# A graph-network layer on one core: norms begun later behind their load, stores issued by ScalarE, four first inputs loaded together, a second lane half a batch behind

## The chip, the cores and the metric

The kernel runs on one core of a Trainium2 chip. The metric is device time in microseconds, median of several runs. The core has a TensorE (matmuls and transposes; PE in the profile, with PEld for its weight loads), a VectorE (DVE), a ScalarE (ACT), a GpSimd (POOL) and a sync engine (SP) that here does nothing but issue transfers. Each engine has its own instruction stream and takes it in order; semaphores make one wait for another.

## The reference

Input x has 32 batches of 512 nodes with 256 channels; adj holds a 512 x 512 mask for each batch. Everything is float32.

```python
h = maximum(layernorm(x), 0)                       # over the channels
out = x + layer(h, adj)

def layer(x, mask):                                # x is h here
    xc = transpose(x, (0, 2, 1))
    c = relu(bn1(conv1d(xc, conv1_w, 0)))          # 1 tap
    c = bn2(conv1d(c, conv2_w, 8))                 # 17 taps
    x_conv = transpose(relu(c + xc), (0, 2, 1))
    s = x @ w_se.T + b_se                          # 3 numbers per node
    dist = |s_n|^2 + |s_m|^2 - 2 s_n.s_m
    A = exp(-dist) * mask
    msg = relu(x @ w_msg.T + b_msg)
    x_nmp = A @ msg
    gi = concat(x_conv, x_nmp) @ w_ih.T + b_ih     # 3 x 256 outputs
    gh = x @ w_hh.T + b_hh
    r, z = sigmoid(gi_r + gh_r), sigmoid(gi_z + gh_z)
    n = tanh(gi_n + r * gh_n)
    return (1 - z) * n + z * x
```

## The kernel before

All the work of a batch lies on 128 partitions; a 512 x 256 array is four chunks of 128 nodes (NT = 4), or, transposed, two halves of 128 channels (ND = 2). A batch passes through these stages, each a Python generator that emits instructions and yields the time it plans for them on TensorE:

- `begin(b)`: `norm_t` transposes the normalized input on TensorE, half by half, into PSUM (`ps_tr`, two buffers), and ScalarE writes it with a ReLU to `hT` (line 241, two buffers). After the second half `hT` is stored to DRAM (`hd`, line 244), for later stages that read it again, and the input of batch b + 2 is loaded into one of two `x_sb` buffers (line 100). Its norm is put on a list at once (line 617).
- `norm(b)`: VectorE takes statistics of the four chunks (lines 213 and 214), GpSimd raises variance + eps to the power -0.5 (line 147, result `rstd`), VectorE subtracts and scales in place (line 221). It is a generator of five pieces, which are taken one at a time between other work.
- `rows(b)`: the 1-tap convolution (`conv1`) into `h1`, for groups of G = 4 batches.
- `graph(lane, b)`: `messages` (four pairs of matmuls, line 519, recorded at line 93; VectorE takes the result out of PSUM at lines 520 and 521), `factors` and `factors_t`, `kernel_exp` (four small matmuls and four exponentials on ScalarE into `at`), `masked` (the mask tile is transposed on TensorE and multiplied in by VectorE, line 570), and `gather` (eight matmuls, result copied by ScalarE to `xnmp`, line 582, and stored to DRAM as `nd`, line 583).
- `convolution`: the 17-tap convolution as 25 matrix products (`ps_c`) for each group of four batches, by an algorithm with fewer multiplications. Its operands come from sums on VectorE (lines 261 and 264), its 25 weight tiles are computed once in the front (`weights_first`, stored to DRAM as `wd`, line 359) and loaded again for each group (line 365). It starts when all 25 are made and the second lane has no batches left.
- `gates(b)`: 48 matmuls with the two gate weights `whh` and `wih` (line 670), with sigmoids and tanh on ScalarE and a mix on GpSimd, then `finish` (transposes back, residual, store).

There are two lanes for graphs. Lane 0 has buffers for the whole run and takes batches 0, 2, 4 and all from 6; lane 1 has batches 1, 3 and 5 and lives in a pool `prep`, which is closed when the convolution starts, so that the `late` pool (gate weights and buffers) can take its space (`late_pools`).

The order of instructions on every engine is written out by a small planner at the end: each stage is a stream with a rate and a starting clock, and the stream with the lowest clock that is ready goes next. After each step `pace` hands VectorE and ScalarE pieces of side work, as far as a credit allows: sums, operands, norms, weight preparation, evacuations. A piece of a norm is taken as soon as the norm is on the list; nothing asks whether its input has landed. All transfers, loads and stores, are issued by the sync engine in program order.

Of the kernel before, what the change touches and what calls it, by code (L numbers as in the profile page):

```python
# [8 lines left out]
F32 = mybir.dt.float32  # L9
# [4 lines left out]
P = 128  # L14
# [17 lines left out]
G = 4  # L32
# [10 lines left out]
def kernel(  # L43
# [27 lines left out]
    nc = tc.nc  # L71
    B, N, D = x.shape
    NT = N // P
# [7 lines left out]
    front = ctx.enter_context(tc.tile_pool(name="front", bufs=2))  # L81
# [13 lines left out]

    XS, HB, HR, XN, XR = {}, {}, {}, {}, {}

    def load(b):
        XS[b] = front.tile([P, NT, D], F32, name="x_sb", bufs=2)
        nc.sync.dma_start(XS[b], x[b].rearrange("(c p) d -> p c d", p=P))  # L100

    def load_row(b):
# [98 lines left out]
    HT = {}  # L201
    HD = {b: dram.tile([P, ND, N], F32, name=f"hd{b}") for b in range(B)}
    ND_ = {(b, d): dram.tile([P, N], F32, name=f"nd{b}_{d}") for b in range(B) for d in range(ND)}

    NORMS = {}

    def norm(b):

        xs = XS[b]
        st = front.tile([P, NT, 6], F32, name="st")  # L210
        mv = front.tile([P, NT, 2], F32, name="mv")
        for c in range(NT):
            nc.vector.bn_stats(st[:, c, :], xs[:, c, :])  # L213
            nc.vector.bn_aggr(mv[:, c, :], st[:, c, :])  # L214
            if c % 2:
                yield
        rstd = front.tile([P, NT], F32, name="rstd")
        rsqrt(rstd, mv[:, :, 1])
        yield
        for c in range(NT):  # L220
            nc.vector.tensor_scalar(
                xs[:, c, :], xs[:, c, :], mv[:, c, 0:1], rstd[:, c : c + 1],
                op0=ALU.subtract, op1=ALU.mult,
            )
            if c % 2:
                yield

    def norm_all(b):
        if b in NORMS:
            for _ in NORMS.pop(b):  # L230
                pass

    def norm_t(b, d):
        xn = XS[b]
        if d == 0:
            norm_all(b)
            HT[b] = front.tile([P, ND, N], F32, name="hT", bufs=2)
        ps = tr.tile([P, N], F32, name="ps_tr")
        for c in range(NT):
            nc.tensor.transpose(ps[:, c * P : (c + 1) * P], xn[:, c, d * P : (d + 1) * P], ident)  # L240
        nc.scalar.activation(HT[b][:, d, :], ps, AF.Relu)  # L241
        if d == ND - 1:
            XS.pop(b)
            nc.sync.dma_start(HD[b], HT[b])

    def conv1(b, o):
        hT = HT[b] if b < G else HR[b]
# [80 lines left out]
    def weights_first():  # L328

        nonlocal made_w  # L330
        outer = [
            taps_of(
                lambda k, i=i: wraw[:, i, :, :, k, :],
                lambda i=i: prep.tile([P, 2, 3, D], F32, name=f"g{i}", bufs=1),
                True,
            )
            for i in range(ND)
        ]
        for j1 in ORDER:
            g = []  # L340
            for o in outer:
                g.append(next(o))
                yield
            inner = [
                taps_of(
                    lambda k, i=i: g[i][:, :, k, :],
                    lambda i=i: prep.tile([P, 2, D], F32, name=f"gg{i}", bufs=2),
                    False,
                )
                for i in range(ND)  # L350
            ]
            for j2 in ORDER:
                w = cv.tile([P, 2, ND, D], F32, name="w", bufs=3)
                for i in range(ND):
                    nc.scalar.activation(
                        w[:, :, i, :], next(inner[i]), AF.Copy, scale=GSCALE[j1] * GSCALE[j2]
                    )
                    yield
                nc.sync.dma_start(WD[made_w], w)
                made_w += 1  # L360

    def weights_again():
# [107 lines left out]
    def convolution():  # L470

        nonlocal at_product
        wg = (w for _ in range(NG) for w in weights_again())
        yield lambda: made_w == 25 and not lanes[1].batches
        late_pools()
        for g in range(NG):
            sums = summed(g)
            next(sums)
            done = None
            for n in range(25):  # L480
                at_product = m = 25 * g + n
                while len(WS) < min(m + 1 + AHEAD_W, 25 * NG):
                    WS.append(next(wg))
                while len(X2) < m + 1:
                    while operand_some() is None:
                        yield lambda: made > g
                w, x2 = WS[m], X2[m].rearrange("p (r v) -> p r v", v=V)
                ps = cps.tile([P, N], F32, name="ps_c")[:, :NZ]
                for o in range(ND):
                    matmul_sum(  # L490
                        ps[:, o * NU : (o + 1) * NU].rearrange("p (b u) -> p b u", u=U),
                        [
                            (w[:, k, i, o * P : (o + 1) * P], x2[:, i * G : (i + 1) * G, k : k + U])
                            for k in range(2)
                            for i in range(ND)
                        ],
                    )
                    if o == 0 and done is not None:
                        sums.send(done)
                    yield 1.71  # L500
                WS[m] = X2[m] = None
                done = ps
            sums.send(done)


    def late_pools():
        nonlocal late, wih, whh
        prep_ctx.close()
        late = ctx.enter_context(tc.tile_pool(name="late", bufs=1))
        whh = late.tile([P, ND, 3 * D], F32, name="whh")  # L510
        wih = late.tile([P, 2 * ND, 3 * D], F32, name="wih")
        nc.sync.dma_start(whh, w_hh)
        nc.sync.dma_start(wih, w_ih)

    wih = whh = None

# [32 lines left out]
    def kernel_exp(lane, at):  # L549

        pss = []
        for c in range(NT // 2):
            pss += [lane.ps(), tr.tile([P, N], F32, name="ps_tr")]
        for c in range(NT):
            k = slice(32 * c, 32 * c + 5)
            nc.tensor.matmul(  # L556
                pss[c], lane.left[k, :], lane.right[k, :], start=True, stop=True,
                tile_position=(32 * c, 0),
            )
        for c in range(NT):  # L560
            nc.scalar.activation(at[:, c, :], pss[c], AF.Exp)
# [11 lines left out]
    def gather(lane, b, msg, at, d):  # L573
        ps = lane.ps()
        for c in range(NT):
            nc.tensor.matmul(  # L576
                ps, msg[:, c, d * P : (d + 1) * P], at[:, c, :], start=(c == 0), stop=(c == NT - 1)
            )
            if c == 1:
                yield 1.73  # L580
        xnmp = front.tile([P, N], F32, name="xnmp", bufs=1)
        nc.scalar.activation(xnmp, ps, AF.Copy)
        nc.sync.dma_start(ND_[b, d], xnmp)
        yield 1.73

    def finish(b, o_sb, c):
# [20 lines left out]
    def begin(b):  # L607

        nonlocal begun
        yield lambda: begun == b and (b < 2 or b - 2 in messaged) and (b - 2 >= G or made_rows >= b - 1)  # L610
        for d in range(ND):
            norm_t(b, d)
            if d == ND - 1:
                begun = b + 1
                if b + 2 < B:
                    load(b + 2)
                    NORMS[b + 2] = norm(b + 2)
            yield 0.55, 2.0 * d

    made_rows = 0  # L620
# [10 lines left out]
    def graph(lane, b):  # L631

        msg = lane.pool.tile([P, NT, D], F32, name="msg", bufs=1)
        at = lane.pool.tile([P, NT, N], F32, name="at", bufs=1)
        for c in range(NT):
            messages(lane, b, msg, c)
            if c == NT - 1:
                factors(lane)
                messaged.add(b)
            yield 0.93, 0.0 if c < NT - 1 else 4.5  # L640
        factors_t(lane)
        yield 0.67, 3.0
        kernel_exp(lane, at)
        yield 1.2, 5.5
        for n in range(NT):
            masked(lane, b, at, n)
            yield 0.55, 1.0 if n < NT - 1 else 2.5
        for d in range(ND):
            yield from gather(lane, b, msg, at, d)
# [147 lines left out]
    def all_graphs(lane):  # L797
        for b in list(lane.batches):
            if b < G:
                yield lambda: begun > b  # L800
            else:
                yield from begin(b)
            yield from graph(lane, b)
        lane.batches = []
# [10 lines left out]
            yield from rows(b)  # L815

    def all_gates():
        yield lambda: late is not None
        for b in range(B):
            yield from gates(b)  # L820

    NORMS[0] = norm(0)
    load(1)
    NORMS[1] = norm(1)
    lanes[0].ask(3)
    lanes[1].ask(2)
    for k0, k1 in ((0, 9), (9, TAPS)):
# [7 lines left out]
        "finish": (all_finishes(), 1e9, -2.0),  # L835
        "rows": (all_rows(), 1e9, -2.0),
        "graphs": (all_graphs(lanes[0]), 63.0, -1.4),
        "other graphs": (all_graphs(lanes[1]), 63.0, -1.4),
        "conv": (convolution(), 85.5, 0.0),
        "gates": (all_gates(), 125.0, 1.1),  # L840
    }
# [77 lines left out]
```

## Time and profile before

| | |
|---|---|
| time, median of 3 | 2545.94 us (2544.59 to 2547.88) |
| span in the profile | 2541.5 us |
| mean granted TensorE clock | 0.952 of full speed |
| VectorE idle before line 213 for an x load | 274.2 us in 25 waits |
| x load, 512 KB | 4.9 us from issue to landing (median) |
| first matmul of the convolution | at 237.86 us |
| first gate matmul | at 446.41 us |
| bytes moved | 292.56 MB, 115 GB/s over the span |

A row of the profile names engine, source line, operation, output and inputs, the count, the busy time and the idle time of the engine just before, with what ended it (the releaser). "L93" is a helper that records every matmul of `matmul_sum`, so messages, 1-tap convolution and the 17-tap products all have it and are told apart by their tiles: `ps_g<-wmsg,hT` (or `ps_acc` in lane 1) are messages, `ps_c` are products. The clock of TensorE is given as a share of full speed for a stretch. The chain that ended last is followed back from the last instruction and says which work set the end.

The run has a front of some 238 us (six graphs, four rows, the weight preparation), a middle in which convolution, graphs and gates are interleaved, and an end from about 2390 us with gates alone.

### The profile page before, as it was taken

How to read it: one execution, taken by the hardware profiler on the slowest of the kernel's cores; microseconds unless marked ns; L12 is line 12 of the kernel's file. 1: busy time of each engine (PE TensorE's matmuls, PEld its weight loads, DVE VectorE, ACT ScalarE, POOL GpSimd, SP SyncE). 2: the span in 40 equal slices, each digit the busy share in tenths (PEclk: the TensorE clock that was granted, in tenths of full speed). 3: DMA queues.
4: the chain of work that ended last, by engine and by line, in shares of the span. 5: the costliest groups of instructions: out<-in, count | busy, mean ns of one | idle time of the engine just before them, and what ended most of it. 6: DMA issues, size and time to landing. Idle time of an engine off the chain costs nothing.

```text
span 2541.5 us, 21847 instructions
## 1 busy us (share of the span) xinstructions
PE 2316.6 (91%) x8224; PEld 1460.6 (57%) x8224; DVE 1181.6 (46%) x1989; ACT 648.3 (26%) x936; POOL 350.4 (14%) x242
## 2 busy tenths in 40 slices
PE   4667998988889998999999998999999999999998
PEld 2335766555556565666556655666666666666543
DVE  4753755444254443545436544445545554565211
ACT  1432223222222322232222411223221311311211
POOL 1000000110011111101102110111111221121222
PEclk8768999999989999999999999999999999999999
DMA  4543444233333333333323333332333332423221
GB/s 168 190 165 137 153 153 157 83 101 115 124 108 104 120 99 108 129 112 116 113 98 125 112 119 114 124 124 78 118 116 103 112 117 91 133 83 100 83 66 33
DMA packets 136312, 292.56 MB, mean 115 GB/s; under 512 B 12432, under 2 KB 61968, under 8 KB 135568
## 3 DMA queue, kind: packets, MB, share of 16 engines
q1 hardware_dynamic: 136208, 291.18, 34.1%
q8 instruction: 65, 1.06, 0.2%
q14 instruction: 39, 0.32, 0.0%
HBM read 227.69 MB, written 63.44 MB: 115 GB/s over the span
## 4 chain that ended last, share of the span: by engine, by line
PE 80%; DVE 7%; DMA 5%; issue 4%; ACT 2%; POOL 1%; SPq 0%; POOLq 0%; ACTq 0%; DVEq 0%
PE ps_acc L670 37%; PE ps_c L93 22%; PE ps_g L576 7%; PE ps_g L93 7%; DMA x_sb<-in_x_dram 5%; PE ps_tr L568 2%; DVE st L213 1%; PE ps_g L556 1%; PE ps_tr L590 1%; PE ps_acc L576 1%; ACT hT L241 1%; DVE mv L214 1%; PE ps_tr L544 1%; PE ps_tr L240 0%; DVE xconv L680 0%
## 5 line engine op out<-in xcount | busy, mean ns | idle before, releaser
L93 PE MATMUL ps_c<-x,w 128*128 128x228 f32 x3200 | 683.1, 361 | 16.4 <-DMA w<-wd 14.4
L93 PEld LDWEIGHTS ps_c<-x,w 128*128 128x128 f32 x3200 | 608.5, 193 | 135.4 <-issue 106.3
L670 PE MATMUL ps_acc<-xconv,wih 128*128 128x512 f32 x768 | 365.5, 599 | 10.5 <-ACT xconv L681 10.5
L670 PE MATMUL ps_acc<-xnb,wih 128*128 128x512 f32 x768 | 361.4, 593 | 0.0
L670 PE MATMUL ps_acc<-hTb,whh 128*128 128x512 f32 x768 | 358.9, 597 | 0.0
L707 POOL TENSOR_TENSOR o_sb<-hTb,r 128x512 f32<-128x512 f32 x64 | 103.6, 1619 | 1446.0 <-ACT r L702 1391.9
L701 DVE TENSOR_TENSOR r<-ps_acc,r 128x512 f32<-128x512 f32 x64 | 44.3, 691 | 474.1 <-PE ps_acc L670 474.1
L93 PE MATMUL ps_g<-wmsg,hT 128*128 128x259 f32 x464 | 143.2, 454 | 110.3 <-DVE aug L521 80.9
L670 PEld LDWEIGHTS ps_acc<-xconv,wih 128*128 128x128 f32 x768 | 143.8, 193 | 147.8 <-issue 132.7
L670 PEld LDWEIGHTS ps_acc<-hTb,whh 128*128 128x128 f32 x768 | 145.0, 192 | 142.1 <-issue 137.6
L670 PEld LDWEIGHTS ps_acc<-xnb,wih 128*128 128x128 f32 x768 | 142.6, 190 | 140.7 <-issue 140.2
L576 PE MATMUL ps_g<-at,msg 128*128 128x512 f32 x464 | 214.5, 601 | 0.6 <-DVE at L570 0.6
L93 PEld LDWEIGHTS ps_g<-wmsg,hT 128*128 128x128 f32 x464 | 101.6, 226 | 151.3 <-issue 136.0
L213 DVE BATCH_NORM_STATS2 st<-x_sb 128x6 f32<-128x256 f32 x128 | 51.6, 403 | 274.2 <-DMA x_sb<-in_x_dram 274.2
L264 DVE SCALAR_TENSOR_TENSOR x<-x,x 128x471 f32<-128x471 f32 (+1 forms) x184 | 168.9, 918 | 3.1
L261 DVE TENSOR_TENSOR x<-x 128x471 f32<-128x471 f32 x200 | 165.8, 846 | 0.1
L576 PEld LDWEIGHTS ps_g<-at,msg 128*128 128x128 f32 x464 | 89.0, 193 | 101.4 <-issue 99.3
L692 DVE SCALAR_TENSOR_TENSOR r<-ps_acc,vec,r 128x512 f32<-128x512 f32 x64 | 48.0, 750 | 211.9 <-PE ps_acc L670 209.5
L570 DVE TENSOR_TENSOR at<-ps_tr,at 128x512 f32<-128x512 f32 x128 | 87.7, 688 | 120.7 <-PE ps_tr L568 113.8
L147 POOL TENSOR_TENSOR rstd<-veps,mhalf 128x4 f32<-128x4 f32 x32 | 38.1, 1190 | 726.4 <-DVE veps L146 726.4
L698 ACT ACTIVATE z<-ps_acc,brz 128x512 f32<-128x512 f32 x64 | 44.0, 687 | 324.2 <-PE ps_acc L670 320.2
L524 ACT ACTIVATE msg<-msg 128x512 f32<-128x512 f32 x64 | 40.2, 628 | 290.6 <-DVE msg L520 290.6
(105 smaller groups left out, 2195.7 us busy)
## 6 DMA issues: line engine op xcount, KB each, us to landing
w<-wd SPq DMA_DIRECT2D x200, 512.0 KB, 3.7
m_sb<-in_adj_dram SPq DMA_DIRECT2D x128, 256.0 KB, 2.7
x_sb<-in_x_dram SPq DMA_DIRECT2D x32, 512.0 KB, 4.9
hd<-hT SPq DMA_DIRECT2D x32, 512.0 KB, 3.0
nd<-xnmp SPq DMA_DIRECT2D x64, 256.0 KB, 2.0
hTb<-hd SPq DMA_DIRECT2D x32, 512.0 KB, 4.5
xnb<-nd SPq DMA_DIRECT2D x64, 256.0 KB, 3.0
res<-in_x_dram SPq DMA_DIRECT2D x64, 256.0 KB, 3.9
```

Of the source, the lines that this page charges most:

```text
L93: nc.tensor.matmul(ps, lhsT, rhs, start=(i == 0), stop=(i == len(pairs) - 1))
L213: nc.vector.bn_stats(st[:, c, :], xs[:, c, :])
L261: nc.vector.tensor_tensor(dst, get(a), get(b), op=ALU.subtract)
L264: nc.vector.scalar_tensor_tensor(dst, a, -2.0, b, op0=ALU.mult, op1=ALU.add)
L568: nc.tensor.transpose(ps[:, c, :], m[:, c * P : (c + 1) * P], ident)
L570: nc.vector.tensor_tensor(part, ps, part, op=ALU.mult)
L576: nc.tensor.matmul(ps, msg[:, c, d * P : (d + 1) * P], at[:, c, :], start=(c == 0), stop=(c == NT - 1))
L670: nc.tensor.matmul(ps, w[:, at + i, cols(o, g)], hT[:, i, :] if k == 0 else x_in[2 * k - 2 + i], start=(k == of[0] and i == 0), stop=(k == ...
L692: nc.vector.scalar_tensor_tensor(r, ps_h, vec[:, _COL["b_hh"] + 2 * ND + o : _COL["b_hh"] + 2 * ND + o + 1], r, op0=ALU.add, op1=ALU.mult,)
L698: nc.scalar.activation(z, ps_z, AF.Sigmoid, bias=brz[:, ND + o : ND + o + 1])
L701: nc.vector.tensor_tensor(r, ps_n, r, op=ALU.add)
L707: nc.gpsimd.tensor_tensor(t, hT[:, o, :], r, op=ALU.subtract)
```

## The change

Four edits, and one number of the planner.

1. A norm is no longer put on the list when its load is issued. `norm_begin` is called after the exponentials of a graph, for the next two batches not yet begun, and by `norm_t` for a batch that nobody has begun. It is meant to let the load land before VectorE meets the norm.
2. The first four inputs are loaded at the start, two of them into the space of lane 1's `at` buffer; so `at` is taken later, and the graphs of batches 0 to 3 wait at that point until batch 3 has been transposed. Batches 4 and 5 are loaded after the transposes of 0 and 1.
3. The stores of `hT`, of `xnmp` and of the prepared weights are issued by ScalarE, which has just written the data, in place of the sync engine.
4. The gate weights are loaded when the convolution has come to product 3, and not ahead of its first weights; the gates stream waits for that.
5. The second lane's clock starts at -1.27 in place of -1.4, half a batch behind the first.

```diff
-    def load(b):
-        XS[b] = front.tile([P, NT, D], F32, name="x_sb", bufs=2)
+    def load(b, xs=None):
+        XS[b] = front.tile([P, NT, D], F32, name="x_sb", bufs=2) if xs is None else xs
...
+    def norm_begin(b):
+        if b < B and b not in normed:
+            normed.add(b)
+            NORMS[b] = norm(b)
...
         if d == 0:
+            if b not in normed:
+                norm_begin(b)
             norm_all(b)
...
-            nc.sync.dma_start(HD[b], HT[b])
+            nc.scalar.dma_start(HD[b], HT[b])
...
-                nc.sync.dma_start(WD[made_w], w)
+                nc.scalar.dma_start(WD[made_w], w)
...
+                if m == 3:
+                    nc.sync.dma_start(whh, w_hh)
+                    nc.sync.dma_start(wih, w_ih)
...
-        nc.sync.dma_start(whh, w_hh)
-        nc.sync.dma_start(wih, w_ih)
...
-        nc.sync.dma_start(ND_[b, d], xnmp)
+        nc.scalar.dma_start(ND_[b, d], xnmp)
...
-                if b + 2 < B:
-                    load(b + 2)
-                    NORMS[b + 2] = norm(b + 2)
+
+                later = b + 4 if b < 2 else b + 2 if b >= G else B
+                if later < B:
+                    load(later)
...
-        at = lane.pool.tile([P, NT, N], F32, name="at", bufs=1)
...
+        if b < G:
+            yield lambda: begun >= G
+        at = lane.pool.tile([P, NT, N], F32, name="at", bufs=1)
         kernel_exp(lane, at)
+        norm_begin(begun)
+        norm_begin(begun + 1)
...
-        yield lambda: late is not None
+        yield lambda: at_product > 3
...
-    NORMS[0] = norm(0)
     load(1)
-    NORMS[1] = norm(1)
+    spare = prep.tile([P, NT, N], F32, name="at", bufs=1).rearrange("p c (k d) -> p (c k) d", d=D)
+    for b in (2, 3):
+        load(b, spare[:, (b - 2) * NT : (b - 1) * NT, :])
+    for b in range(G):
+        norm_begin(b)
...
-        "other graphs": (all_graphs(lanes[1]), 63.0, -1.4),
+        "other graphs": (all_graphs(lanes[1]), 63.0, -1.27),
```

More of the change, by code (lines that the diff above doesn't have):

```diff
@@ L203 @@
     ND_ = {(b, d): dram.tile([P, N], F32, name=f"nd{b}_{d}") for b in range(B) for d in range(ND)}
-    NORMS = {}
+    NORMS, normed = {}, set()
+    def norm_begin(b):
+        if b < B and b not in normed:
+            normed.add(b)
+            NORMS[b] = norm(b)
     def norm(b):
```

## The prediction

> **What bounds the kernel now.** I read the shares of busy time first, then the table of stretches, the waits, the chain that ended last, and one stall in order of time.
>
> ```profile
> PE 2316.6 (91%) x8224; PEld 1460.6 (57%) x8224; DVE 1181.6 (46%) x1989; ACT 648.3 (26%) x936; POOL 350.4 (14%) x242
> PEclk8768999999989999999999999999999999999999
> ```
>
> TensorE is the bound, 91% busy; what can be won is its 225 us of idle time and the time it runs at a reduced clock. Both are early: the slices of the clock below 9 are the first four and one more. Two 40 us stretches of the middle, with a stall and without (columns: busy us and count of PE, PEld, DVE, ACT, POOL, then clock, DMA share, GB/s):
>
> ```profile
> 270.00:310.00 40.00, 34.06 (x148) 27.20 (x147) 24.89 (x48) 7.36 (x14) 1.32 (x1) 0.91 0.36 125
> 350.00:390.00 40.00, 40.00 (x172) 28.28 (x171) 15.64 (x18) 11.44 (x19) 0.00 (x0) 1.00 0.42 147
> ```
>
> Where there is no stall, PE has no idle time at all and the full clock. The waits, whole run (us in total, times, longest):
>
> ```profile
> DVE st L213 <- DMA x_sb<-in_x_dram: 274.2, 25, 22.2
> PE ps_g L93 <- DVE aug L521: 80.9, 17, 7.3
> PE ps_g L93 <- DVE veps L146: 29.4, 5, 6.8
> PE ps_tr L540 <- issue: 16.4, 1, 16.4
> PE ps_c L93 <- DMA w<-wd: 14.4, 1, 14.4
> PE ps_acc L93 <- DVE veps L146: 10.6, 1, 10.6
> PE ps_acc L670 <- ACT xconv L681: 10.5, 5, 4.7
> ```
>
> The message matmuls (line 93, called from line 519) wait 110 us in 22 pieces for VectorE to free their PSUM, and VectorE waited 25 times for an x load. The timeline shows that these are one thing (start us, length, engine, line, operation, then idle before it and its releaser):
>
> ```profile
> 280.02 0.32 SPq L244 DMA_DIRECT2D hd<-hT  x1
> 280.43 0.38 SPq L100 DMA_DIRECT2D x_sb<-in_x_dram  x1
> ...
> 282.12 1.92 PE L93 MATMUL ps_g<-wmsg,hT 128*128 128x259 f32 x8
> 285.32 0.43 DVE L213 BATCH_NORM_STATS2 st<-x_sb 128x6 f32<-128x256 f32 x1 [12.04 <-DMA x_sb<-in_x_dram]
> ...
> 289.35 0.42 DVE L520 TENSOR_TENSOR msg<-ps_g,bmsg 128x256 f32<-128x256 f32 x1
> ...
> 289.98 3.79 PE L93 MATMUL ps_g<-wmsg,hT 128*128 128x259 f32 x8 [5.94 <-DVE aug L521]
> ```
>
> The load is issued at 280.43. The norm's first instruction follows it in VectorE's program and blocks VectorE until 285.3; then come 2.1 us of statistics and some sums, and only at 289.35 does VectorE take the messages out of PSUM. PE stands 5.94 us, and then 8 matmuls take 3.79 us, where the 8 before the stall took 1.92. The chain that ended last counts the load itself as 5% of the span and lines 213 and 214 as 1% each.
>
> **What the Trainium skill says.** "TensorE: Matmul & The Clock Gate", Part 1: about 3.4 us of idle time takes the array to half clock, and about 3.4 us of activity brings it back. The trace agrees: 474 ns for a message matmul after the stall, 240 before it. The same page, "Architectural detail", says that VectorE and ScalarE are strict FIFO; the 12.04 us that VectorE sat before line 213 with ready sums behind it agree. "DMA: Bandwidth & Descriptors", "Issuing engines are not separate DMA queues": issuing from another engine saves only sequencer time. On the sync queue one issue takes 0.32 us (the hd row above); no row of before shows one on ScalarE. The same page, "Queues, rings and completion order": sync and scalar have a row of rings each, served in turn, so a store from ScalarE need not stand behind queued loads. The page of before has only one such queue, so no run shows it yet.
>
> **The change part by part.**
>
> (1) Norms begun later. In steady state the norm of b+2 is now begun after the exponentials of graph b, and its load is still issued after the transposes of b. Between them lie four message matmul pairs, the factors and the exponential with two planned gaps: over 20 us in the stall above (load at 280.4, exponentials of that graph after 302). A load takes 4.9 us to land (median), so VectorE no longer blocks. No instruction is removed: 4 statistics of 0.40 us, 4 aggregates of 0.18, 4 scalings of 0.41 and one of 0.17, 4.1 us, go in elsewhere, among masks and gathers, and one block of graphs lies between them and their first use. Removed from PE between 238 and 1900 us: of the 22 waits one (6.5 us) lies in the front and two (1.7, 1.5) follow no load; 110.3 - 9.7 = 100.6 us in 19 stalls. The cold clock after one: 3.79 - 1.92 = 1.9 us on the messages, and the 24 products after them 5.64 us in the chain against 4.62 for 24 later: 1.0. Other stalls show 1.2 to 3; I take 2.5, so 19 x 2.5 = 48. Together at most 148. The control is in the trace: the graph of batch 30, which starts no load, has its messages at 1784 to 1799 us with no PE idle time at all. That of batch 31 loses 1.5 us, because VectorE was behind with wide sums. Such queueing will come back: between 230 and 430 us VectorE is busy 29.0 + 34.4 + 26.4 + 35.3 = 125 of 200 us, and in a stretch shorter by four stalls of 8 us it is 75%. I charge 12%: 130 us are won.
>
> (2) Four inputs loaded at the start. Loads 2 and 3 go ahead of masks and convolution weights. In before the third was issued at 15.1 behind 4.3 MB of weights and took 14.0 us, and PE stood 10.6 us. By then 8 MB had landed in some 28 us, some 290 GB/s, so four inputs and the small weights (2.7 MB) land by about 11 us and the weights only 3 us later, still before their first use at 57.9. Saved: 10.6 us, and of the 16.4 us stall after it, which holds VectorE's wait for the fifth input (5.8) and its statistics (2.3) but also 10 us of weight arithmetic, some 3. The price is that loads 2 and 3 sit in the buffer of the second lane's exponentials, so both graphs 0 and 1 are held until batch 3 is transposed. In before that point (51 us) also lay ahead of the exponentials (76 us): nothing. In the last pair of graphs before the convolution the waits of 6.5 and 2.8 us and a cold start go: 10. Waits of VectorE alone (8.0 at 76 us) give perhaps 3.
>
> (3) Stores from ScalarE's queue: 32 of hT, 64 of xnmp, 25 of w, 121 issues. At the 0.32 us of the sync queue that is 39 us more on an engine that is busy 648 of 2541; bounds are 0 and 0.5 us each (60). Queued behind the issue are ReLUs, sigmoids and PSUM copies; PE waits for ScalarE only 10.5 + some 12 us in all, so I take nothing off for it. The sync queue loses head-of-line waits for ScalarE (423.9 us for xnmp, 91 for hT), so x, mask and w loads behind them leave earlier.
>
> (4) Gate weights loaded at product 3. In before 2.3 MB stand ahead of the first w; it lands 10.3 us after its issue, where w has a median of 3.7, and it was itself queued behind stores of the last graph. PE stood 14.4 us. With both gone, I take 3 us left: 11 won. The 2.3 MB then stand ahead of the w of product 6, which has three products (10 us and graph work) to land, so that is hidden. Gates first run at 446 us.
>
> (5) Second lane half a batch behind: no work added; it takes apart two graphs that wait for the same engines at the same steps. Counted in (2).
>
> Sum: 130 + 13.6 + 10 + 3 + 11 = 168 us; 2546 - 168 = 2378. The end of the kernel (from 2390 gates alone, with 15 us of idle time) doesn't change.
>
> **The rivals.**
>
> A, part of it comes back. The waits are exchanged: norms now stand between mask multiplications, whose PSUM (two buffers) PE needs, or the scaling waits for a GpSimd power behind three 1.6 us products of the gates. For it: VectorE at 75%, and rstd waits today (20.3 us in 21 waits). Against: none of those is longer than 1.2 us. If half of the 148 is kept and a third of the 38: 2546 - 74 - 12 = 2460.
>
> B, slower. The x load is late anyway, as the sync queue stands behind a w load (613.7 us of such waits), so the stall moves from messages to masks, and 121 issues of 0.32 us on ScalarE come on top: 2546 + 39 = 2585. Against: the w load ahead in the queue waits for a product that PE has run before the transposes, and the load left 0.4 us after the store in every row I read.
>
> C, better. The middle loses all 148, and the stagger also takes the front's mask steps (0.8 to 1.4 us of waiting each) and its half clock: 60 there in place of 38. 2546 - 208 = 2338.
>
> **How the numbers follow.** Main case 0.6, A 0.2, B 0.05, C 0.15. Prediction 2378. The low end lies just under C, 2332; the high end at A, 2460, which leaves out B, half of A and a little below C, under 2 in 10. Main, A and C are all faster: 0.95, with 0.02 for a cancellation and 0.03 slower, the rest of B being a smaller loss of the same kind that other gains cover.
>
> **What would show it.** Right: VectorE's wait of line 213 on the load falls from 274 us to under 40; the messages' wait on line 521 and 146 from 110 to under 25; the clock of the stretches between 270 and 1900 us is 0.98 or more; the first product begins at about 200 us, in place of 238; ScalarE's busy time is unchanged and a second hardware queue appears. Wrong: new PE waits in place of the old ones (line 568 on line 570, line 570 behind rstd: A), waits on masks with line 213 still on the load (B), a longer front than 238 us, or ScalarE named as releaser for more than 40 us of PE.

## The result and the profile after

The changed kernel takes 2350.39 us (median of 4, 2348.49 to 2352.06) against 2545.44 us: ratio 0.9232, 95% interval 0.9216 to 0.9248, 195 us faster. Measured once more with the later experiments (e8) it gave 0.9239 (0.9226 to 0.9252). The page after, busy time and the clock in 40 slices:

```profile
PE 2263.6 (96%) x8224; PEld 1428.0 (61%) x8224; DVE 1200.0 (51%) x1989; ACT 651.7 (28%) x936; POOL 353.6 (15%) x242
PEclk8889999999999999999999999999999999999999
```

The same 8224 matmuls take 53 us less busy time (2316.6 before): that is clock, since no matmul was taken out (the granted clock is 0.984 of full speed, 0.952 before). ScalarE's busy time has not moved, because issues of transfers are not counted in it. The waits after, whole run (us, times, longest):

```profile
PE ps_tr L247 <- DVE x_sb L226: 11.5, 1, 11.5
...
PE ps_g L93 <- DVE aug L529: 10.9, 7, 3.4
...
PE ps_tr L548 <- DVE at L578: 8.6, 1, 8.6
PE ps_tr L564 <- ACT hT L248: 8.4, 1, 8.4
...
PE ps_tr L576 <- DMA m_sb<-in_adj_dram: 6.5, 3, 2.7
...
DVE st L218 <- DMA x_sb<-in_x_dram: 0.6, 1, 0.6
```

VectorE's wait for an x load has gone from 274.2 us to 0.6, and the messages' waits on VectorE from 110 us to under 12. What is left on top belongs to the front. One graph after the change, where before stood the stall at 290 us (timeline: start, length, engine, line, operation):

```profile
264.18 0.38 SPq L100 DMA_DIRECT2D x_sb<-in_x_dram  x1
265.48 0.33 ACTq L251 DMA_DIRECT2D hd<-hT  x1
...
267.06 3.71 PE L93 MATMUL ps_g<-wmsg,hT 128*128 128x259 f32 x16
268.14 0.42 DVE L528 TENSOR_TENSOR msg<-ps_g,bmsg 128x256 f32<-128x256 f32 x1 [2.34 <-PE ps_g L93]
...
280.11 0.60 ACT L569 ACTIVATE at<-ps_g 128x512 f32<-128x512 f32 x1 [2.04 <-PE ps_tr L564]
...
281.24 0.41 DVE L218 BATCH_NORM_STATS2 st<-x_sb 128x6 f32<-128x256 f32 x1
```

Load, messages without a gap (16 matmuls in 3.71 us, where 8 took 3.79 after the stall), exponentials, and only then the statistics, 17 us behind the load and with no idle time ahead of them. The stretch from 270 to 310 us:

```profile
270.00:310.00 40.00, 40.00 (x174) 29.52 (x173) 31.09 (x54) 9.55 (x18) 1.27 (x1) 1.00 0.55 190
```

PE is busy for all 40 us at full clock, where it was 34.06 at 0.91. VectorE does more in it (31.1 us, 24.9 before) and holds nobody up.

Where the time came from, split at the first matmul of the convolution and at the last (PE idle time summed from the timeline of each kernel):

| | before | after |
|---|---|---|
| first product at, us | 237.86 | 198.32 |
| from there to the end, us | 2303.6 | 2152.0 |
| PE idle: front / middle / end, us | 92.2 / 117.2 / 11.2 | 54.5 / 16.6 / 11.2 |

So 39.5 us were won in the front and 151.6 behind it. The second profile of the same kernel (e8) has its first product at 195.94 us and 2152.4 us behind it. A difference of 2 or 3 us in the time of the first product is therefore no more than two executions of one kernel show; the part behind it agreed within 0.4 us.

### The profile page after: what moved, and what is told of

Read it like the earlier page. It is cut to its first block, busy times and chain, and to the rows that moved or that the text cites. A ratio compares the mean times of both kernels' runs of the same rounds, so it can differ in the third digit from the quotient of the medians.

```text
span 2350.3 us, 21846 instructions
## 1 busy us (share of the span) xinstructions
PE 2263.6 (96%) x8224; PEld 1428.0 (61%) x8224; DVE 1200.0 (51%) x1989; ACT 651.7 (28%) x936; POOL 353.6 (15%) x242
## 3 DMA queue, kind: packets, MB, share of 16 engines
q10 hardware_dynamic: 17424, 46.67, 5.2%
## 4 chain that ended last, share of the span: by engine, by line
PE 91%; DVE 5%; ACT 1%; issue 1%; DMA 1%; POOL 0%; ACTq 0%; SPq 0%; POOLq 0%; DVEq 0%
PE ps_acc L683 41%; PE ps_c L93 25%; PE ps_g L584 8%; PE ps_g L93 8%; PE ps_tr L576 2%; PE ps_g L564 1%; PE ps_tr L598 1%; PE ps_tr L247 1%; DVE y L387 1%; PE ps_tr L552 1%; PE ps_acc L584 1%; DVE xconv L693 1%; ACT w L362 1%; DMA m_sb<-in_adj_dram 1%; DVE x L268 0%
## 5 line engine op out<-in xcount | busy, mean ns | idle before, releaser
L93 PE MATMUL ps_c<-x,w 128*128 128x228 f32 x3200 | 672.8, 356 | 4.4 <-issue 4.4
L93 PEld LDWEIGHTS ps_c<-x,w 128*128 128x128 f32 x3200 | 597.9, 190 | 122.1 <-issue 110.1
L93 PE MATMUL ps_g<-wmsg,hT 128*128 128x259 f32 x464 | 119.5, 398 | 10.1 <-DVE aug L529 10.1
L93 PEld LDWEIGHTS ps_g<-wmsg,hT 128*128 128x128 f32 x464 | 89.4, 198 | 44.8 <-issue 31.8
L528 DVE TENSOR_TENSOR msg<-ps_g,bmsg 128x256 f32<-128x256 f32 x116 | 48.9, 422 | 126.6 <-PE ps_g L93 125.9
L721 POOL TENSOR_TENSOR o_sb<-z,o_sb 128x512 f32<-128x512 f32 x64 | 111.6, 1744 | 5.0
```

The costliest lines, as they stand in the source:

```text
L93: nc.tensor.matmul(ps, lhsT, rhs, start=(i == 0), stop=(i == len(pairs) - 1))
L528: nc.vector.tensor_tensor(msg[:, c, :], ps[:, :D], bmsg[:, :D], op=ALU.add)
L721: nc.gpsimd.tensor_tensor(t, z, t, op=ALU.mult)
```

## The experiments

My theory is that of the forecast: VectorE, in order, stood before a norm whose load had not landed, and everything behind it with it. The rival was that the stores on ScalarE's queue bring the gain, because they clear the sync queue for the loads; a second, that the place of the norm's 4 us of work matters and not the wait. Ratios are to the kernel before, on the same chip. Times in text are medians.

**e1: the first edit alone, on the kernel before.**

```diff
-                    NORMS[b + 2] = norm(b + 2)
...
         kernel_exp(lane, at)
+        norm_begin(begun)
+        norm_begin(begun + 1)
```

> The kernel before with the first edit alone: a norm is begun after a graph's exponentials, everything else as before. If VectorE being blocked by a load that has not landed is the main cost (theory), the middle wins its 100 us of PE waits and most of 48 us of half clock and the front little: 2390 to 2410 us, and VectorE's wait on the x load before the statistics falls below 60 us, what is left of it in the front. If the stores on ScalarE's queue are the main thing, since they let loads out of the sync queue earlier (rival), the load lands as late as before and this kernel stays above 2500 us.

2384.12 us, ratio 0.9373 (0.9360 to 0.9387): 157 of the 195 us, 6 us below the lower end of my band. No wait of VectorE for an x load is left in its profile. The page shows that all transfers still go through one queue; the messages' row after e1, then that row before (busy, mean ns, idle just before):

```profile
L93 PE MATMUL ps_g<-wmsg,hT 128*128 128x259 f32 x464 | 115.2, 389 | 9.9 <-DVE aug L528 9.9
```

```profile
L93 PE MATMUL ps_g<-wmsg,hT 128*128 128x259 f32 x464 | 143.2, 454 | 110.3 <-DVE aug L521 80.9
```

100 us of idle time and 28 us of busy time leave this one row, and I read the second number as the half clock of its first matmuls: the mean of one falls from 454 to 389 ns, and the stall shown in the prediction had 474 ns behind it and 240 ahead. The stretch from first product to end, before and in e1 (columns: stretch, PE, PEld, DVE, ACT, POOL busy, clock, DMA share, GB/s):

```profile
237.86:2541.50 2303.64, 2171.38 (x7770) 1379.96 (x7770) 1061.99 (x1691) 574.98 (x803) 335.49 (x215) 0.97 0.33 109
```

```profile
216.45:2383.20 2166.75, 2129.90 (x7770) 1350.31 (x7770) 1083.18 (x1704) 573.83 (x803) 341.42 (x216) 1.00 0.34 116
```

The same 7770 matmuls: 136.9 us less, of which 41.5 are busy time (clock) and 95.4 idle time. The front gives 21.4 us, where I had expected little.

**e2: the first edit undone in the changed kernel.**

```diff
                 if later < B:
                     load(later)
+                    norm_begin(later)
...
-        norm_begin(begun)
-        norm_begin(begun + 1)
```

> The changed kernel with the first edit undone: a norm goes on the list when its load is issued, all else stays. Theory: the stalls of the middle come back, 19 or so with 5 us of PE idle and 2.5 us of half clock each, so 2480 to 2505 us, with VectorE waiting about 200 us for x loads after the front. Rival (stores on ScalarE): most of the gain stays, below 2400 us.

2478.39 us, ratio 0.9743 (0.9727 to 0.9760): 128 us are lost again, and the time is 2 us under my band. In the profiles 107 of them lie behind the first product, which comes at 216.24 us, 17.9 later. One of its stalls:

```profile
443.62 0.38 SPq L100 DMA_DIRECT2D x_sb<-in_x_dram  x1
...
448.22 0.43 DVE L218 BATCH_NORM_STATS2 st<-x_sb 128x6 f32<-128x256 f32 x1 [14.37 <-DMA x_sb<-in_x_dram]
...
452.90 3.79 PE L93 MATMUL ps_g<-wmsg,hT 128*128 128x259 f32 x8 [4.30 <-DVE aug L529]
```

With the stores on ScalarE the picture is that of before: 192.8 us of VectorE waiting for x loads in all. e1 and e2 together refute the first rival.

**e3: the three stores back on the sync engine.** All three `nc.scalar.dma_start` of the changed kernel become `nc.sync.dma_start`.

> The changed kernel with all 121 stores on the sync engine again. Theory: they were never on the path; 2345 to 2362 us. Rival: sync's waits for ScalarE come back ahead of x, mask and weight loads, and the time goes above 2450 us. A third case, that 121 issues of 0.33 us on ScalarE cost something, would make this kernel faster than 2340 us.

2361.07 us, ratio 0.9283 (0.9270 to 0.9297), 11 to 13 us slower than the changed kernel: far from the rival, just inside the theory's band, yet not nothing. The first product waits for its weights again. The sync queue of e3, and then the first product:

```profile
192.30 4.31 SPq L591 DMA_DIRECT2D nd<-xnmp  x2
196.66 1.40 SPq L372 DMA_DIRECT2D w<-wd  x3
```

```profile
200.28 3.41 PE L93 MATMUL ps_c<-x,w 128*128 128x228 f32 x8 [4.70 <-DMA w<-wd]
```

The weight load stands behind the last stores of xnmp, which wait for ScalarE; in the changed kernel it leaves at 181.46 us. The profiles put 2 us of the loss before the first product, which is within the scatter, and 6 behind it, where the idle time is the same and PE's busy time is longer. The changed kernel's first product has no wait ahead of it:

```profile
198.32 1.70 PE L93 MATMUL ps_c<-x,w 128*128 128x228 f32 x8
```

The same 8 matmuls take 3.41 us in e3. Over the first 10 us the clock of e3 is 0.55, that of the changed kernel 1.00, and from the first product to the first gather behind it the same instructions take 22.8 us in place of 18.4. So 4.4 of the 6 us are the reduced clock after the wait for the weights; the rest was not traced.

**e4: both lanes at -1.4 again.**

```diff
-        "other graphs": (all_graphs(lanes[1]), 63.0, -1.27),
+        "other graphs": (all_graphs(lanes[1]), 63.0, -1.4),
```

> The changed kernel with the second lane's clock back at -1.4. Only the order in the front differs, before the first product at 198 us. If the stagger helps as meant, the front loses waits of 1 to 3 us in mask steps and exponentials, 5 to 15 us in all: 2355 to 2365 us. If it does nothing, 2348 to 2352 us.

2369.70 us, ratio 0.9322 (0.9309 to 0.9334): some 20 us slower, 5 us above my band. Its stretch from first product to end, and that of the changed kernel:

```profile
200.87:2367.70 2166.83, 2129.40 (x7770) 1350.76 (x7770) 1082.07 (x1704) 576.91 (x803) 341.37 (x216) 1.00 0.35 118
```

```profile
198.32:2350.30 2151.98, 2120.26 (x7750) 1346.03 (x7748) 1076.43 (x1680) 575.97 (x800) 339.79 (x215) 1.00 0.36 118
```

The stagger hardly moves the first product (2.5 us, with a 5.9 us wait for weights inside). It moves work: with the second lane behind, the first has gone on to batch 6 in the front's gaps, and 20 matmuls fewer stand behind the first product. There, 9 us of busy and 6 us of idle time are less, but the moved work is only part of that. Its matmuls (messages and factors) take 4.4 us in e4. Another 2.2 us are reduced clock after the wait for weights: e4's first 16 products take 5.48 us, 16 later ones 3.25. The other 2.5 us of busy time and the idle time, which lies in small waits of at most 1.8 us, are not explained by these runs.

The wait for weights is explained by the order of the sync queue, in e4 and then in the changed kernel:

```profile
195.01 0.38 SPq L100 DMA_DIRECT2D x_sb<-in_x_dram  x1
195.52 1.73 SPq L372 DMA_DIRECT2D w<-wd  x3
```

```profile
180.41 0.38 SPq L100 DMA_DIRECT2D x_sb<-in_x_dram  x1
...
181.46 1.94 SPq L372 DMA_DIRECT2D w<-wd  x3
```

The weight load stands behind the x load, and this one waits (16.4 us in e4) until the first lane has transposed batch 6 and its buffer is free. When that lane is further on, both leave 14 us earlier.

**e5: gate weights ahead of the first convolution weights.** The two loads move from product 3 back to the opening of their pool, and the gates stream waits for that again.

> The changed kernel with the gate weights loaded as soon as their space is free, ahead of the first convolution weights. As forecast, the 2.3 MB add about 7 us to the landing of the first weights: 2356 to 2360 us, with PE waiting 5 us or more before the first product. If the weights of the first products are not what PE waits for there, 2349 to 2352 us.

2364.62 us, ratio 0.9298 (0.9285 to 0.9310), 15 us slower, more than the band allowed; in the trace the first product comes at 206.98 us behind an 11.37 us wait for its weights, 8.7 us later than in the changed kernel, and 2.8 us more follow behind it, at a clock of 0.50 in the first 10 us.

**e6: two inputs at the start, two after the transposes of 0 and 1.** No spare space, no hold.

```diff
-                later = b + 4 if b < 2 else b + 2 if b >= G else B
+                later = b + 2
```

> The changed kernel with two inputs at the start and the next two after the transposes of 0 and 1, no spare space and no hold of the graphs of 0 to 3. As forecast, the third input then waits behind 4.3 MB of weights, and the norms of batches 2 and 3 are begun when they are needed, with VectorE blocked: 10 to 25 us longer, 2360 to 2375 us. If the hold of the exponentials cost as much as the early loads win: 2345 to 2355 us.

2358.95 us, ratio 0.9275 (0.9263 to 0.9288), between the two cases. The first waits of its front:

```profile
33.62 2.30 PE L247 MATMUL ps_tr<-ident,x_sb 128*128 128x128 f32 x8 [4.74 <-DVE x_sb L226]
...
54.78 2.25 PE L247 MATMUL ps_tr<-ident,x_sb 128*128 128x128 f32 x8 [11.51 <-issue]
```

16 us of waiting at the third and fourth input stand against 8.4 us that the changed kernel waits at its exponentials (49.5 us) on ScalarE. There ScalarE stands behind the first wide weight sums of VectorE (its copy of the first weights waits 7.07 us for them). The 11.51 us at the fourth input of e6 have the same cause: VectorE has no idle time ahead of that input's statistics, which follow these weight sums. The first product is 4.9 us later; the profiled run was the shortest of e6, 2354.19 us.

**e7: the norm at its old place, but for an input that has landed.**

```diff
                 if later < B:
                     load(later)
+                norm_begin(b + 1)
...
-        norm_begin(begun)
-        norm_begin(begun + 1)
```

> The changed kernel with the norm begun at its old place, right after the load is issued and ahead of the messages, but for batch b+1, whose input landed one graph ago, and not for b+2. Theory (the wait for the load costs, not the place of the 4.1 us of work): 2345 to 2360 us. Rival (the norm's work ahead of the messages is itself what holds up PSUM): 1.5 to 3 us of PE waiting for each of 26 graphs, 2390 to 2430 us.

2343.59 us, ratio 0.9216 (0.9203 to 0.9229), no slower than the changed kernel, and its first product comes at 190.80 us. The messages of the first lane wait 4.3 us for line 529 and 2.2 for line 146 in the whole run, those of the second 3.1. So the place of the work, right ahead of the messages, costs nothing that these runs show; a norm begun before its load has landed is the cost. The second rival falls.

**e8 to e11: what is left in the front.** e8 is the changed kernel again, the mark for the others.

> The changed kernel once more, unedited, as the mark for the three that follow and for the repeat of its ratio: 0.922 to 0.925 of before.

2349.93 us, 0.9239 (0.9226 to 0.9252). The other three are edits of e7.

```diff
-        Lane(front, 3, (gps, "ps_g"), [0, 2, 4, *range(6, B)]),
-        Lane(prep, 2, (acc, "ps_acc"), [1, 3, 5]),
+        Lane(front, 4, (gps, "ps_g"), [0, 2, 4, *range(6, B)]),
+        Lane(prep, 3, (acc, "ps_acc"), [1, 3, 5]),
...
-    lanes[0].ask(3)
-    lanes[1].ask(2)
+    lanes[0].ask(4)
+    lanes[1].ask(3)
```

> The kernel with the norm of a landed input at the old place, and one mask buffer more in each lane (4 and 3). In the front PE waits 8.5 us in three pieces for mask tiles that were asked for only when a buffer came free. Theory: these waits go, 5 to 10 us faster than the kernel with the landed norm alone (0.9216), 0.918 to 0.920 of before. If the extra 512 KB ahead of the convolution weights delays the weight preparation: no gain or a loss, 0.921 to 0.925.

e9: 2335.35 us, ratio 0.9183 (0.9167 to 0.9199), the fastest of all. PE no longer waits for a mask (8.5 us in e7), and the first product comes at 180.64 us in place of 190.80.

In e10 the second lane starts at -1.14.

> The kernel with the landed norm and the second lane a whole batch behind (-1.14). Half a batch was worth 20 us. If what counts is work of the first lane done in the front's gaps, some 5 to 10 us more are won, 0.918 to 0.920. If the first product is only put off by the longer second lane, 0.922 to 0.930.

e10: 2353.93 us, ratio 0.9257 (0.9244 to 0.9270), slower than e7: the first product comes 16.5 us later (207.35), and only 23 more matmuls have been done ahead of it (499 against 476). Of my two cases this is the one in which the first product is only put off: work done ahead in the front is not won in full, and half a batch was better than a whole one.

In e11 only the second lane is held until batch 3 is transposed.

> The kernel with the landed norm, and the hold of the exponentials until batch 3 is transposed for the second lane alone, whose buffer is borrowed. PE waits 8.4 us at that point for ScalarE, which stands behind weight sums. If the hold makes this wait: 4 to 9 us faster than 0.9216, 0.918 to 0.920. If the weight sums make it wherever the exponentials stand: 0.921 to 0.923.

e11: 2346.03 us, ratio 0.9226 (0.9211 to 0.9241), not told apart from e7, and PE waits the same 8.5 us. The hold doesn't make that wait.

## Why the prediction was right

The time, 2350 us, lies in the range, 28 us under the 2378 of the main case; the mechanism was the forecast one. By its own terms:

- **Norms later, middle (130 us forecast).** e1 isolates it: 136.9 us, 95.4 of idle time (forecast 100.6) and 41.5 of clock (forecast 48). The charge of 12% for queueing was too large: 136.9 of 148 came. Of what did not, some 5 us are idle time; the rest was never there, as a stall cost 2.2 us of clock (41.5 over 19) and not 2.5. After the change the messages lose 10.9 us in 7 pieces, and only one, 3.45 us at 820 us, is long. VectorE, busy for 81% of the stretch from 230 to 310 us and 68% from 230 to 430, did not bring the waits back.
- **Early inputs (13.6 us), last pair (10) and other waits (3).** Mis-attributed: e1, without early inputs, already moves the first product by 21.4 us, and undoing the first edit in the changed kernel (e2) moves it back by 17.9. Undoing the early inputs costs 4.9 us at the first product in the trace of the shortest run of e6 and 9 to 11 us in the ratio. The wait at the fourth transposes that I had mostly put down to weight sums did stay, as 8.4 us at the exponentials.
- **Gate weights at product 3 (11 us).** 8.7 us at the first product and some 15 us in all (e5). It needs the stores on ScalarE and the stagger with it: without one of them the weights again leave late, behind the last xnmp stores (e3) or behind an x load (e4). PE then waits for them 4.7 and 5.9 us, and 11.4 in e5. The three losses overlap and cannot be added. Gates first run earlier than the 446 us I gave: at 425.2 us before and 364.8 after, which still leaves 154 us to weights that are asked for at 210.88.
- **Stores on ScalarE (nothing taken off).** An issue takes 0.33 us there, close to the 0.32 of the sync queue that I used; no wait on it stands out. That they win 11 to 13 us was only in my account through the first weights, and what the traces show won there is not the time of an issue but the wait of the sync queue for ScalarE ahead of them.
- **Stagger (counted in the front, no term of its own).** This is the term that failed. I had it as a way to shorten the front's waits and gave a further worth to it only in rival C. It is worth 20 us (e4), 15 of them behind the first product: some 4 are matmuls that the first lane does ahead in the front's gaps, some 2 the clock after a wait for weights that goes with it, and the rest is open.

The sum: the front gave 39.5 us for 37.6 forecast, but from other parts, so that this agreement is luck; the middle 151.6 for 130, of which 15 are the stagger (e4) and 7 the overcharge (e1). Of the rivals, A (half of it comes back in mask steps) is refuted by the middle's 16.6 us of idle time: the scaling waits for rstd 24.9 us in 17 pieces, the longest now 5.8 us in place of 1.2, so its mechanism exists but is small. B is refuted by the 0.6 us that VectorE waits for loads. The weight loads in the sync queue did not make x late: the load at 264.18 us left 1.3 us ahead of its own batch's hT store. The other signs came as well: a second hardware queue carries 46.67 MB, ScalarE is the releaser for some 22 us of PE's idle time, and of the 40 us stretches between 270 and 1900 us one alone has a clock below 0.98 (0.91 at 790 to 830, around the one long wait). Of C, most of the middle's gain and the stagger's worth came; its extra in the front did not.

## What to carry to other kernels

An in-order engine must not be given work on a transfer in the same breath as the transfer: give it the input loaded one round earlier, or put the work behind something that takes longer than the load; where in the round the work then stands hardly matters (e1, e7). Price such a stall at the idle time of the engine that is the bound and the half clock after it: here 95 and 41 us. Where a phase is bound by latency, work of the next one in its gaps can pay even when the phase ends no earlier, but it has to be tried how far: half a batch won 20 us (e4), a whole one lost 10 against it (e10), and only some 4 of the 20 us are the moved matmuls. A load on the path can stand in its queue behind another transfer that waits for an engine (e3, e4): look at what is ahead of it.

## What the hardware showed that I had not expected

A 512 KB hT store took 6.2 us to land (median) from ScalarE's queue and 3.0 from the sync queue. In the graph shown from ScalarE it leaves 1.3 us behind the x load, in the one shown from the sync queue 0.4 us ahead of it. The queue alone is not the reason: the four hT stores from ScalarE that have no x load within 8 us of them (batches 2, 3, 30 and 31) landed in 2.6 to 3.4 us, the other 28, each with an x load within 4.3 us, in 4.3 to 8.4. In all but one of the 28 the x load leaves first. That it delays the store fits this; other loads of the same moments were not separated from it. No wait in the changed kernel's profile names this store. The 256 KB xnmp stores landed in 2.0 us from either.
